# Layer 1's folded queries: a second level of Strassen in four of seven products, for seven of eight batch elements

## The chip, the cores and the metric

The kernel runs on one core of a Trainium2 chip. The metric is the device time of one execution in microseconds; the time before is the median of three runs. The profile is of one further execution. Everything is float32.

## The reference, cut to what matters

Two attention layers over eight images of 512 channels and 1024 pixels. The change touches layer 1:

```python
h = _group_norm(x, gamma, beta).reshape(B, C, N)          # C = 512, N = 1024
q = jnp.einsum('oc,bcn->bon', wq, h) + bq[None, :, None]
k = jnp.einsum('oc,bcn->bon', wk, h) + bk[None, :, None]
v = jnp.einsum('oc,bcn->bon', wv, h) + bv[None, :, None]
logits = jnp.einsum('bcn,bcm->bnm', q, k) * scale
attn = jax.nn.softmax(logits, axis=-1)
o = jnp.einsum('bnm,bcm->bcn', attn, v)
out = jnp.einsum('oc,bcn->bon', wp, o) + bp[None, :, None]
return x + out.reshape(B, C, H, W)
```

Layer 0 is a layer norm over channels, attention with eight heads of 64, an output projection and the residual.

## The kernel before

**Folded weights.** In layer 1 the product wq^T wk is formed once ("a") and the keys are h itself: the queries qa are one 512 x 512 matrix times h, plus a vector `ua`. Values and output projection are folded as well ("m").

**Strassen.** Each large product is one level of Strassen: a matrix is four blocks of 256 rows, with the sums S1 to S4 of the weights and T1 to T4 of the operands (Winograd's form). `STEPS` gives the order of the seven products and the bank that each goes to; a step with False adds onto what is in the bank:

```python
STEPS = [("11", "11", "x", True), ("12", "21", "z", True), ("S2", "T2", "x", False), ("S1", "T1", "y", True),
         ("S3", "T3", "x", False), ("S4", "22", "y", False), ("22", "T4", "x", False)]
```

`Product` runs them: `multiply()` puts matmuls on TensorE; `leave()` then copies x or y out (ScalarE, before the next step adds onto it) or adds a bank and a copy into the result (VectorE, `out`, L386). So steps 0, 2, 3 and 6 end in a copy u(0, 0), u(0, 1), u(1, 1) or the block (1, 0), and steps 1, 4 and 5 in an out. Between the two, `step()` calls `tick(pieces)`.

**A second level.** The scores (`Whole.scores`, L1160) are `SINGLES`, six outer products, each of them seven inner ones of 128 x 128 x 512 by the same steps, and the seventh outer product (22 with T4, L1195) whole. They run as three pairs of units. Inner sums of the operands are made by `deep_operands_later` (L558 to L563), those of the queries by `Whole.deep_query` (L1134 to L1140). Layer 0's keys and queries are done likewise (`project_deep`, L588), with inner sums of the weights made once, saved to DRAM (`save_deep_later`) and loaded for each element (`load_deep`).

**The queries before.** `project` makes two units, one for each 128 rows of a block. Each of the seven products is whole: 4 matmuls of 128 x 128 x 512 in all, 2 to a unit (L481). In between, two steps of the next element's layer-0 values (unit `n_units[1]`, L490) take the time in which group norm and the T sums are made (`meanwhile`).

**Order.** PE, ACT, DVE and POOL run their instructions in the order in which the program is written; DMAs on SP have a queue of their own. POOL can run ahead of the others where nothing holds it. Work that has no fixed place goes through one first-in first-out queue of closures, `side`: `later()` puts entries at its end, a `tick` runs one, and `until()` runs entries until what is needed exists. Which step an entry lands in is a matter of counting.

**From scores to the softmax's sums.** After each pair of scores, entries add the outer products together (`adds`, L1200), `finish` takes the exponentials of a block (L1148), `key_sum` adds its two halves on VectorE (L1250), `more_sums` adds the other blocks by accumulating DMAs of POOL (L1255), and `fold` folds the 128 partitions by further ones (L720, L716). `inverse` turns them on VectorE (L724) and spreads the rows on ScalarE (L1294). The next element's layer norm goes on behind it (L797). While this runs, the folded values (`project_v`, x_vm, y_vm, z_vm, L490) and the product with the attention (x_o, y_o, z_o, L506) are on TensorE, and the v units take the ticks (2, 2, 2, 2, 1, 1, 1) and (1, 1, 1, 2, 1, 2, 2).

**Stores.** `put_away` stores the next element's layer-0 values to DRAM (v_away), `residual` adds the folded output bias to the residual x1 on ScalarE (L1538) and stores it (x_away, L1539). `LayerNorm.sums` adds the next but one input over its channels by POOL's DMAs (L753). All tiles of 4 KB a partition come from one pool of 46.

Of the kernel before, what the change touches and what calls it, by code (L numbers as in the profile page):

```python
# [20 lines left out]
P = 128  # L21
# [50 lines left out]
def fast_path(ctx: ExitStack, tc: tile.TileContext, x: bass.AP, vecs: dict, weights: dict, out: bass.AP,  # L72
# [139 lines left out]
    saved_deep = {n: dram.tile([P, 3, 2, 4, P], F32, tag=f"saved_deep_{n}", name=f"saved_deep_{n}") for n in ("k", "q")}  # L212
# [4 lines left out]
    def load_deep(n, b):  # L217
        ready = {}
        for g in range(3):
# [5 lines left out]
    def save_deep_later(n, w):  # L225
# [18 lines left out]
        for g in range(3):  # L244
            sums(g)

    def save_w(n, w):
# [99 lines left out]
    def later(*work):  # L347
        side.extend(work)
# [198 lines left out]
    def operand_inner(h, deep, names):  # L547
# [2 lines left out]
        return Inner(blocks, lambda: [{t: deep[x][:, i] for i, t in enumerate(order)} for x in names],  # L550
                     lambda: all(x in deep for x in names))

    def deep_operands_later(h, deep, names):

        def first(n):
            x = h[n]
            t = made[n] = big_tile(f"{n}_deep_{h['tag']}").rearrange("p (i t) -> p i t", i=4)
            nc.vector.tensor_sub(t[:, :2], x[:, :, CB:], x[:, 0, :].rearrange("p (n t) -> p n t", n=2))  # L558

        def rest(n):  # L560
            x, t = h[n], made[n]
            nc.vector.tensor_add(t[:, 2], t[:, 1], x[:, 0, :CB])
            nc.vector.tensor_sub(t[:, 3], x[:, 1, :CB], t[:, 2])  # L563
            deep[n] = t

        made = {}
        for n in names:
            later(lambda n=n: first(n), lambda n=n: rest(n))

    def project_deep(tag, w, w_deep, bias, h, h_deep, pieces):  # L570
# [44 lines left out]
        def run():  # L615
# [47 lines left out]
            res["last"] = last  # L663
            yield
        return run(), res

    def rows_of(t, c, k):

# [443 lines left out]
    class Whole:  # L1112
# [3 lines left out]
        def __init__(self, b, qa, hb, x1):  # L1116
            self.b, self.hb, self.x1 = b, hb, x1
            self.q_deep = {}
            self.pieces = (2, 2, 1)
            self.q = {f"{i + 1}{j + 1}": qa[j, i] for i in range(2) for j in range(2)}  # L1120
# [5 lines left out]
            for n in names:  # L1126
                sum_later(self.q, n, lambda n: block(f"{n}_qa_{self.b}"), wide)

        def deep_query(self, *names):
# [12 lines left out]

            made = {}
            for n in names:
                later(lambda n=n: first(n), lambda n=n: rest(n))

# [3 lines left out]
        def scores(self, h_deep):  # L1150
# [51 lines left out]
            def adds(ts_, xs):  # L1202
                later(*(lambda g=g: add(ts_[g], xs[g]) for g in range(2)))

            def finish(n, t):
                def exponentials():
                    for g in range(2):
                        self.exponential(t[g])
                    self.p[n] = t
                later(exponentials)  # L1210

            for j in range(3):
                units = [unit(2 * j + n) for n in range(2)]
                for i in range(len(STEPS)):
                    for u in units:
                        u.multiply()
                    copy = plain(j, i - 3) if j < 2 and i in (3, 4) else nothing
                    tick(self.pieces[j])
                    for u in units:
                        u.leave()  # L1220
                    copy()
                m1, m2, m3, m5, m4, m7 = made
                if j == 0:
                    adds(m2, m1)
                    finish("11", m2)
                elif j == 1:
                    self.key_sum(0, "11")
                    adds(m3, m1)
                    adds(m5, m3)
                    adds(whole6, m5)  # L1230
                    finish("12", whole6)
                else:
                    adds(m3, m4)
                    adds(m7, m3)
                    self.key_sum(1, "12")
                    later(lambda: add(m5[0], m4[0]))
                    finish("21", m7)
# [148 lines left out]
    with tc.manual_schedule(engines=ORDERED):  # L1386
# [62 lines left out]
        for u in units:  # L1449
            u.pieces = 2  # L1450
            u.rest()
        save_deep_later("q", wq_now)
        units, vts = project_v("v0", wv_now, hb)
        for u in units:
            u.pieces = 2
            u.rest()
        for b in range(B):
# [51 lines left out]
            o_units[1].step(2)  # L1509
            o_units[0].rest()  # L1510
            wa_now = load_w("a", b)
            gn = GroupNorm(b, x1, stats)
            if not more:
                until(lambda: not side)
# [19 lines left out]
            def residual(i, k):  # L1534
# [3 lines left out]
                    nc.scalar.activation(t[:, r, :], t[:, r, :], AF.Identity, bias=bm[:, oc : oc + 1])  # L1538
                nc.sync.dma_start(out=x1_away[i, k], in_=wide(t))  # L1539
            h1b = operands(h1)  # L1540
            if more:
                add_operands(h1b)
            a_units, qa = project(f"qa{b}", wa_now, lambda oc: ua[:, oc : oc + 1], h1b,
                                  own="x" if more else "")
            if not more:
# [8 lines left out]
            a_units[0].step(1)  # L1554
            meanwhile(3)
            a_units[0].step(1)
            if more:
                vn_away = {ik: put_away(t, f"v_away_{b + 1}_{ik[0]}{ik[1]}") for ik, t in vn.items()}
            a_units[1].step(2)
            ln = LayerNorm(b + 2) if b + 2 < B else None  # L1560
            if ln:
                ln.sums()
            h1_deep = {}
            away = list(x1)
            for n, (_, name) in enumerate(SINGLES):
                deep_operands_later(h1b, h1_deep, [name])
                later(*(lambda ik=ik: residual(*ik) for ik in away[n : n + 1]))
            for u in a_units:
                u.pieces = 2
            a_units[0].rest()  # L1570
            whole = Whole(b, qa, h1b, x1_away)
            whole.deep_query("11")
            a_units[1].step(5)
            whole.deep_query("12")
            whole.query_sum("S1", "S2")
            whole.deep_query("S2")
            whole.query_sum("S3")
# [445 lines left out]
```

## Time and profile before

| | |
|---|---|
| Median of three runs | 2820.01 us (2818.68 to 2821.12) |
| Profiled execution, its own time | 2816.65 us |
| Its span | 2814.4 us |
| Granted TensorE clock | 1.00 |
| PE busy | 2801.8 us |
| DVE busy | 2066.1 us |
| ACT busy | 1233.8 us |
| POOL busy | 502.0 us |
| One element's queries, element 0 | from 280.44 to 307.92 us |
| Its scores | from 307.92 to 351.05 us |

Times in the rows of the profile are microseconds from the span's start; in the groups' rows the mean duration is in ns. Matmuls overlap in the records, so what one costs is read from the distance between starts. A float32 matmul leaves two records, each with a weight load on PEld.

### The profile page before, as it was taken

To read this page: it belongs to the slowest core of one execution; us is meant where nothing else is said; L and a number is where in the kernel's file an instruction comes from. 1 tells how busy PE (TensorE), PEld (TensorE's weight loads), DVE (VectorE), ACT (ScalarE), POOL (GpSimd) and SP (SyncE) were. 2 spreads that over 40 slices of the span, in tenths; PEclk is the share of its full clock that TensorE was granted. 3 is DMA by queue.
4 is the path that set the end of the run, shared out by engine and by line. 5 is a ranking of instruction groups with operands and counts; after the bars stand their busy time and mean duration, and the time that the engine had idled before them with its cause. 6 is when DMAs were issued, how large, how long until landed. Compare 5 with 4: busy or idle time off the path is not lost.

```text
span 2814.4 us, 31060 instructions
## 1 busy us (share of the span) xinstructions
PE 2801.8 (100%) x10807; PEld 1596.2 (57%) x10807; DVE 2066.1 (73%) x2892; ACT 1233.8 (44%) x2079; POOL 502.0 (18%) x685
## 2 busy tenths in 40 slices
PE   9999999999999999999999999999999999999999
PEld 5535656357553575535854457644676346663375
DVE  6677777777767776777767777678767777657785
ACT  4463435724257242662436523365234733236341
POOL 2021022210222102220032200222012210122001
PEclk9999999999999999999999999999999999999999
DMA  8234267352663527535374353734337432372214
GB/s 315 93 82 110 79 166 185 68 131 86 156 170 72 144 82 182 128 78 165 89 188 96 91 152 92 200 78 114 123 98 202 99 85 86 71 206 63 65 64 99
DMA packets 133765, 341.38 MB, mean 121 GB/s; under 512 B 18928, under 2 KB 23328, under 8 KB 133600
## 3 DMA queue, kind: packets, MB, share of 16 engines
q0 software_dynamic: 53760, 127.45, 24.7%
q1 hardware_dynamic: 79744, 211.84, 21.1%
q8 instruction: 87, 1.43, 0.2%
q14 instruction: 78, 0.64, 0.1%
q10 hardware_dynamic: 96, 0.02, 0.0%
HBM read 190.87 MB, written 62.39 MB: 90 GB/s over the span
## 4 chain that ended last, share of the span: by engine, by line
PE 94%; DMA 3%; DVE 1%; issue 1%; ACT 0%; POOL 0%; ACTq 0%; POOLq 0%; DVEq 0%
PE s L1003 16%; PE acc L1021 16%; PE s L1160 7%; PE x_o L506 6%; PE x_v L490 4%; PE x_qa L481 4%; PE x_out L481 4%; PE x_vm L490 3%; PE y_s L1160 3%; PE y_o L506 3%; PE y_v L490 2%; PE y_out L481 2%; PE s L1195 2%; PE x_q L588 2%; PE y_qa L481 2%; PE y_vm L490 2%
## 5 line engine op out<-in xcount | busy, mean ns | idle before, releaser
L1012 DVE TENSOR_TENSOR sum<-sum,p 128x1024 f32<-128x1024 f32 x384 | 470.4, 1225 | 39.4 <-DVE sum L1012 1.4
L1006 ACT ACTIVATE p<-s 128x1024 f32<-128x1024 f32 (+1 forms) x608 | 478.9, 983 | 15.1 <-PE s L1003 15.1
L1021 PE MATMUL acc<-p,v_again 128*64 128x512 f32 x1792 | 390.9, 594 | 0.0
L1021 PEld LDWEIGHTS acc<-p,v_again 128*64 128x64 f32 x1792 | 126.1, 137 | 261.4 <-issue 236.7
L716 POOL DMA_DIRECT2D fold<-sum x312 | 207.6, 757 | 302.4 <-DMA sum<-sum 187.0
L1003 PE MATMUL s<-q,k 64*128 64x512 f32 x1152 | 252.2, 592 | 0.0
L1003 PE MATMUL s<-q_lower,k_lower 64*128 64x512 f32 x896 | 196.1, 592 | 0.0
L1010 DVE TENSOR_TENSOR sum<-p,p 128x1024 f32<-128x1024 f32 x64 | 78.1, 1221 | 157.8 <-ACT p L1006 157.8
L1003 PEld LDWEIGHTS s<-q,k 64*128 64x128 f32 x1152 | 109.6, 186 | 138.4 <-issue 84.6
L1255 POOL DMA_DIRECT2D sum<-p x32 | 28.5, 970 | 864.6 <-PE y_vm L490 757.2
L1003 PEld LDWEIGHTS s<-q_lower,k_lower 64*128 64x128 f32 x896 | 85.4, 186 | 110.5 <-issue 68.5
L720 POOL DMA_DIRECT2D sum<-sum x78 | 66.2, 849 | 419.1 <-DVE sum L1012 239.6
L1025 ACT COPY o<-acc 128x512 f32<-128x512 f32 x63 | 36.9, 586 | 221.2 <-PE acc L1021 221.0
L1200 DVE TENSOR_TENSOR p<-p,p 128x1024 f32<-128x1024 f32 x112 | 131.7, 1216 | 0.0
L506 PE MATMUL x_o<-T_p,S_vm 128*128 128x512 f32 x256 | 115.2, 592 | 0.0
L511 ACT COPY u(0, 0)_v<-x_v 128x512 f32<-128x512 f32 x16 | 9.4, 586 | 186.5 <-PE x_v L490 186.5
L490 PE MATMUL x_vm<-w_m,T_gn 128*128 128x256 f32 x384 | 90.7, 379 | 0.0
L481 PE MATMUL x_qa<-T_gn,w_a 128*128 128x512 f32 x192 | 89.4, 594 | 0.8 <-ACT qa L524 0.8
L481 PE MATMUL x_out<-T_o,w_o 128*128 128x512 f32 x192 | 89.2, 594 | 0.0
L506 PEld LDWEIGHTS x_o<-T_p,S_vm 128*128 128x128 f32 x256 | 48.6, 190 | 60.7 <-issue 60.7
L1067 ACT COPY rr<-r 32x16 f32<-32x16 f32 x256 | 53.5, 209 | 62.4 <-DVE r L970 59.0
L490 PE MATMUL x_v<-w_v,T_h 128*128 128x256 f32 x336 | 80.0, 381 | 0.0
(524 smaller groups left out, 5317.9 us busy)
## 6 DMA issues: line engine op xcount, KB each, us to landing
sum<-sum POOLq DMA_DIRECT2D x78, 256.0 KB, 3.4
fold<-sum POOLq DMA_DIRECT2D x312, 64.0 KB, 2.4
x<-in_x_dram SPq DMA_DIRECT2D x32, 512.0 KB, 5.4
xr<-in_x_dram SPq DMA_DIRECT2D x64, 256.0 KB, 5.0
x_away<-x SPq DMA_DIRECT2D x32, 512.0 KB, 2.7
sum<-p POOLq DMA_DIRECT2D x32, 512.0 KB, 5.9
v_away<-v SPq DMA_DIRECT2D x28, 512.0 KB, 3.3
v_again<-v_away SPq DMA_DIRECT2D x28, 512.0 KB, 9.2
```

The costliest lines, as they stand in the source:

```text
L481: nc.tensor.matmul(dst, a[:, k, ts(r, P)], b[:, k, :], start=(opens and k == 0), stop=(k == 1), skip_group_check=True)
L490: nc.tensor.matmul(dst[:, ts(m, CB)], b[:, k, ts(2 * r + m, P)], a[:, k, :], start=(opens and m == 0 and k == 0), stop=(k == 1), skip_grou ...
L506: nc.tensor.matmul(dst, a[:, m, ts(r, P)], b[m // 2][:, m % 2, :], start=(opens and m == 0), stop=(m == NM // 2 - 1), skip_group_check=True)
L716: nc.gpsimd.dma_start(out=f[ts(q + i, BL), :], in_=t[ts(n, BL), ts(i, HB)], accum_op=ALU.add if n else ALU.bypass)
L720: nc.gpsimd.dma_start(out=t[:D, :], in_=t[D:, :], accum_op=ALU.add)
L1003: nc.tensor.matmul(parts[i], self.k[m // 4][r, ts(m % 4, P)], self.q[r, :], start=True, stop=True)
L1006: nc.scalar.activation(dst, src, AF.Exp, scale=1.0 / float(D) ** 0.5)
L1010: nc.vector.tensor_add(self.sum, self.p[0], p)
L1012: nc.vector.tensor_add(self.sum, self.sum, p)
L1021: nc.tensor.matmul(acc[i * D : (i + 1) * D, :], value_of(self.vt, m, self.c * P + i * D, D), self.p[m][:, ts(i, HB)], start=(m == 0), stop ...
L1160: nc.tensor.matmul(dst[:, ts(c, CB)], x[0][:, ts(c, P)], a[0], start=(opens and c == 0), stop=True, skip_group_check=True)
L1200: nc.vector.tensor_add(wide(t), wide(t), wide(x))
```

## The change

For elements 0 to 6 the queries go through a new `project_mixed`. Three outer products stay whole (m1 = 11 with 11, m2 = 12 with 21, m6 = 22 with T4); the other four (S2 with T2, S3 with T3; S1 with T1, S4 with 22) are done as two units of two, each outer product by seven inner ones of 128 x 128 x 256. The order on every engine is written out in it. The inner sums of the operands, which the scores need as well, are made here (`Primes`), and the residual's stores are placed here (`beside`). The last two blocks of the queries (22 and 21) are summed by entries of `side` (`closing`). Inner sums of the weights S1, S2, S3, S4 are made once, saved, and loaded for each element. In the scores of all eight elements, the sums of the first pair go to POOL's DMAs, and the exponentials of block 11 and its key sum change their place. Element 7 keeps `project`.

```diff
+        for g in groups:
...
+    class Primes:
+        def __init__(self, h):
+            self.h, self.deep = h, {}
+        def first(self, n):
+            x = self.h[n]
+            t = self.deep[n] = big_tile(f"{n}_deep_{self.h['tag']}").rearrange("p (i t) -> p i t", i=4)
+            nc.vector.tensor_sub(t[:, :2], x[:, :, CB:], x[:, 0, :].rearrange("p (n t) -> p n t", n=2))
+            nc.vector.tensor_add(t[:, 2], t[:, 1], x[:, 0, :CB])
+        def last(self, n):
+            t = self.deep[n]
+            nc.vector.tensor_sub(t[:, 3], self.h[n][:, 1, :CB], t[:, 2])
...
+    def project_mixed(tag, w, w_deep, bias, h, primes, between, away, beside, ready):
+        n_blocks = {n: block(f"{tag}_{n}") for n in ("m1", "m2", "m6")}
+        banks = {n: wide_psum(f"{n}_{tag}") for n in "cab"}
+        made = [[None, None], [None, None]]
+        def products(n, r, t):
+            a, x = {"m1": ("11", "11"), "m2": ("12", "21"), "m6": ("22", "T4")}[n]
+            for k in range(2):
+                nc.tensor.matmul(banks[t][:, ts(r, HB)], w[a][:, k, ts(r, P)], h[x][:, k, :], start=(k == 0),
+                                 stop=(k == 1), skip_group_check=True)
+        def biased(n, r, t, i):
+            nc.scalar.activation(n_blocks[n][:, r, :], banks[t][:, ts(r, HB)], AF.Identity, bias=bias(2 * i + r))
+        def part(dst, a, x, opens):
+            for s in range(2):
+                nc.tensor.matmul(dst[:, ts(s, CB)], a[s], x[s], start=(opens and s == 0), stop=True,
+                                 skip_group_check=True)
...
+        def step(u, *work):
+            u.multiply()
+            for x in work:
+                x()
+            u.leave()
...
+            later(lambda: sums(c22, "22", q22), nothing, nothing, nothing, lambda: sums(c12, "21", q21))
+        def c12(r):
+            nc.vector.scalar_tensor_tensor(q21[:, r], mc[r][:, 1], bias(r), mb[r][:, 0], ALU.add, ALU.add)
+        def c22(r):
+            nc.vector.scalar_tensor_tensor(q22[:, r], mc[r][:, 0], bias(2 + r), mb[r][:, 1], ALU.add, ALU.add)
+        products("m1", 0, "c")
+        add_operand(h, "T1")
+        between()
+        add_operand(h, "T2")
+        products("m1", 1, "c")
+        beside()
+        add_operand(h, "T3")
+        between()
+        nc.scalar.copy(wide(n_blocks["m1"]), banks["c"])
+        away()
+        primes.first("T2")
+        primes.first("T3")
+        beside()
+        for r in range(2):
+            products("m2", r, "b")
+        biased("m2", 0, "b", 0)
+        B, C_ = unit(0), unit(1)
+        m1, m2, m6 = (n_blocks[n] for n in ("m1", "m2", "m6"))
+        primes.first("T1")
+        primes.first("22")
+        primes.last("T2")
+        primes.last("T3")
+        step(B)
+        biased("m2", 1, "b", 0)
+        nc.gpsimd.dma_start(out=wide(m2), in_=wide(m1), accum_op=ALU.add)
+        step(B)
+        step(B, t("T4"))
+        beside()
+        step(C_, last("T1", "22"))
+        step(B, first("21"))
+        step(C_, last("21"))
+        beside()
+        step(B)
+        step(C_, first("11"), last("11"))
+        step(B)
+        products("m6", 0, "c")
+        biased("m6", 0, "c", 1)
+        step(B, lambda: ready(m2))
+        step(C_)
+        mb, mc = made
+        step(C_)
+        pairs(lambda r: add(mb[r][:, 0], m1[:, r]))()
+        products("m6", 1, "c")
+        biased("m6", 1, "c", 1)
+        step(C_, pairs(lambda r: add(mb[r][:, 1], mb[r][:, 0])), pairs(lambda r: add(m6[:, r], mb[r][:, 1])))
+        step(C_)
+        for r in range(2):
+            nc.gpsimd.dma_start(out=mb[r][:, 0], in_=mc[r][:, 0], accum_op=ALU.add)
...
                 if j == 0:
-                    adds(m2, m1)
+                    for g in range(2):
+                        nc.gpsimd.dma_start(out=wide(m2[g]), in_=wide(m1[g]), accum_op=ALU.add)
+                elif j == 1:
                     finish("11", m2)
-                elif j == 1:
-                    self.key_sum(0, "11")
                     adds(m3, m1)
                     adds(m5, m3)
                     adds(whole6, m5)
+                    self.key_sum(0, "11")
                     finish("12", whole6)
...
             wa_now = load_w("a", b)
+            if more:
+                wa_deep = load_deep("a", b, (1, 2))
...
+                def vn_put_away():
+                    for ik, t in vn.items():
+                        vn_away[ik] = put_away(t, f"v_away_{b + 1}_{ik[0]}{ik[1]}")
+                    if ln:
+                        ln.sums()
...
+                def ready(t):
+                    whole.q["11"] = t
+                    whole.query_prime("11")
+                qa, closing = project_mixed(f"qa{b}", wa_now, wa_deep, lambda oc: ua[:, oc : oc + 1], h1b, primes,
+                                            lambda: n_units[1].step(1), vn_put_away,
+                                            lambda: residual(*spare.pop(0)), ready)
+                whole.q["12"] = qa[1, 0]
+                whole.deep_query("12")
+                closing(whole.q)
```

More of the change, by code (lines that the diff above doesn't have):

```diff
@@ L210, in load_w, with load_deep @@
         return w
-    saved_deep = {n: dram.tile([P, 3, 2, 4, P], F32, tag=f"saved_deep_{n}", name=f"saved_deep_{n}") for n in ("k", "q")}
+    saved_deep = {n: dram.tile([P, 3, 2, 4, P], F32, tag=f"saved_deep_{n}", name=f"saved_deep_{n}") for n in ("k", "q", "a")}
     def deep_tile(n, b, g):
         return big_tile(f"w_{n}_{b}_{g}_deep").rearrange("p (s i o) -> p s i o", s=2, i=4)
-    def load_deep(n, b):
+    def load_deep(n, b, groups=range(3)):
         ready = {}
-        for g in range(3):
+        for g in groups:
             deep = deep_tile(n, b, g)
@@ L223, in load_deep, with save_deep_later @@
         return ready
-    def save_deep_later(n, w):
+    def save_deep_later(n, w, groups=range(3)):
         def sums(g):
@@ L242, in sums @@
                   lambda: nc.gpsimd.dma_start(out=saved_deep[n][:, g], in_=made[0]))
-        for g in range(3):
+        for g in groups:
             sums(g)
@@ L665, in project_deep, with unit, dest, bank_of @@
         return run(), res
+    def project_mixed(tag, w, w_deep, bias, h, primes, between, away, beside, ready):
[13 more added lines that the diff above has]
+                                 skip_group_check=True)
+        def unit(j):
+            def dest(i, k):
+                if made[j][i] is None:
+                    made[j][i] = big_tile(f"{tag}_{j}{i}").rearrange("p (s t) -> p s t", s=2)
+                return made[j][i][:, :, ts(k, CB)]
+            def bank_of(to):
+                if to == "y":
+                    return bank(f"y_{tag}_{j}")
+                return banks["c"][:, ts(j, HB)] if to == "z" else banks["ab"[j]][:, :HB]
+            a, x = ((("S2", "S3"), ("T2", "T3")), (("S1", "S4"), ("T1", "22")))[j]
+            u = Product(f"{tag}_{j}", weight_inner(w, w_deep, a), operand_inner(h, primes.deep, x), part, plain_shift,
+                        dest, bank_of)
+            u.view = lambda t: t.rearrange("p (s t) -> p s t", s=2)
+            return u
+        def step(u, *work):
[3 more added lines that the diff above has]
+            u.leave()
+        def t(n):
+            return lambda: add_operand(h, n)
+        def first(n):
+            return lambda: primes.first(n)
+        def last(*names):
+            return lambda: [primes.last(n) for n in names]
+        def add(dst, src):
+            nc.vector.tensor_add(dst, dst, src)
+        def pairs(work):
+            return lambda: [work(r) for r in range(2)]
+        def closing(q):
+            def sums(f, n, t):
+                for r in range(2):
+                    f(r)
+                q[n] = t
+            later(lambda: sums(c22, "22", q22), nothing, nothing, nothing, lambda: sums(c12, "21", q21))
[49 more added lines that the diff above has]
+        step(C_)
+        for r in range(2):
+            nc.gpsimd.dma_start(out=mb[r][:, 0], in_=mc[r][:, 0], accum_op=ALU.add)
+        q21, q22 = (block(f"{tag}_{n}") for n in ("21", "22"))
+        return {(1, 0): m6}, closing
@@ L1119, in __init__ @@
             self.pieces = (2, 2, 1)
-            self.q = {f"{i + 1}{j + 1}": qa[j, i] for i in range(2) for j in range(2)}
+            self.q = {f"{i + 1}{j + 1}": qa[j, i] for i in range(2) for j in range(2) if (j, i) in qa}
             self.p = {f"{j + 1}{k + 1}": [None, None] for j in range(2) for k in range(2)}
@@ L1127, in query_sum, with query_prime, query_primes @@
                 sum_later(self.q, n, lambda n: block(f"{n}_qa_{self.b}"), wide)
-        def deep_query(self, *names):
+        def query_prime(self, n):
+            first, rest = self.query_primes()
+            first(n)
+            rest(n)
+        def query_primes(self):
             def first(n):
@@ L1143, in deep_query @@
             made = {}
+            return first, rest
+        def deep_query(self, *names):
+            first, rest = self.query_primes()
             for n in names:
@@ L1452, in fast_path @@
         save_deep_later("q", wq_now)
+        save_deep_later("a", wa, (1, 2))
         units, vts = project_v("v0", wv_now, hb)
@@ L1540, in fast_path @@
             h1b = operands(h1)
+            ln = LayerNorm(b + 2) if b + 2 < B else None
+            primes = Primes(h1b)
+            h1_deep = primes.deep
             if more:
[L1542 to L1545, printed above, removed]
+                def vn_put_away():
[3 more added lines that the diff above has]
+                        ln.sums()
+                vn_away = {}
+                spare = list(x1)
+                whole = Whole(b, {}, h1b, x1_away)
+                def ready(t):
[7 more added lines that the diff above has]
+                closing(whole.q)
+            else:
+                a_units, qa = project(f"qa{b}", wa_now, lambda oc: ua[:, oc : oc + 1], h1b, own="")
                 h1b["T1"] = t1
@@ L1553, in fast_path @@
                 add_operands(h1b)
[L1554 to L1574, printed above, removed]
+                a_units[0].step(2)
+                a_units[1].step(2)
+                away = list(x1)
+                for n, (_, name) in enumerate(SINGLES):
+                    deep_operands_later(h1b, h1_deep, [name])
+                    later(*(lambda ik=ik: residual(*ik) for ik in away[n : n + 1]))
+                for u in a_units:
+                    u.pieces = 2
+                a_units[0].rest()
+                whole = Whole(b, qa, h1b, x1_away)
+                whole.deep_query("11")
+                a_units[1].step(5)
+                whole.deep_query("12")
             whole.query_sum("S1", "S2")
```

## The prediction

> **What bounds the kernel now.** I read the page first (engines, then the 40 slices), then the order of time around the queries of element 0, then the waits of TensorE, then the chain that follows the layer-1 scores.
>
> ```profile
> span 2814.4 us, 31060 instructions
> ...
> PE 2801.8 (100%) x10807; PEld 1596.2 (57%) x10807; DVE 2066.1 (73%) x2892; ACT 1233.8 (44%) x2079; POOL 502.0 (18%) x685
> ...
> PEclk9999999999999999999999999999999999999999
> ```
>
> TensorE has 12.6 us of gaps in 2814.4, at full clock: only less matmul time, or a new wait, can move the end. Two shapes matter (a float32 matmul leaves two records):
>
> ```profile
> 292.47 1.88 PE L481 MATMUL y_qa<-T_gn,w_a 128*128 128x512 f32 x4
> 294.19 1.88 PE L481 MATMUL x_qa<-T_gn,w_a 128*128 128x512 f32 x4
> ...
> 307.92 3.62 PE L1160 MATMUL s<-qa,gn 128*128 128x256 f32 x16
> 311.38 1.03 PE L1160 MATMUL s<-11_deep_qa,11_deep_gn 128*128 128x256 f32 x4
> ```
>
> Durations overlap; starts do not. Four records of 512 columns take 294.19 - 292.47 = 1.72 us, 0.429 each; sixteen of 256 take 311.38 - 307.92 = 3.46, 0.216 each.
>
> Where an engine is 100% busy, the thinnest cover is what to look for. It is behind the scores: the softmax sums go through POOL's DMAs, one waiting for another.
>
> ```profile
> 358.26 0.91 POOL L1255 DMA_DIRECT2D sum<-p  x1 [84.59 <-PE y_vm L490]
> 365.08 1.77 POOL L1255 DMA_DIRECT2D sum<-p  x2 [5.90 <-PE x_vm L490]
> 374.18 0.87 POOL L1255 DMA_DIRECT2D sum<-p  x1 [7.32 <-DMA sum<-p]
> ...
> 388.33 1.61 POOL L716 DMA_DIRECT2D fold<-sum  x2 [1.41 <-DMA fold<-sum]
> ```
>
> ```profile
> 391.61 0.71 DVE L724 STREAM_TRANSPOSE fold1t<-fold 128x512 f32<-128x512 f32 x1 [1.70 <-DMA fold<-sum]
> ```
>
> ```profile
> 394.13 1.70 ACT L1294 COPY rr<-r 32x16 f32<-32x16 f32 x8 [0.91 <-DVE r L970]
> 395.88 1.70 ACT L797 COPY lnmur<-lnm 32x16 f32<-32x16 f32 x8
> 397.60 0.59 ACT L511 COPY u(1, 1)_o<-y_o 128x512 f32<-128x512 f32 x1
> ```
>
> ```profile
> PE y_k L588 <- ACT u(1, 1)_k L602: 1.2, 2, 1.0
> ...
> PE y_o L506 <- ACT u(1, 1)_o L511: 0.4, 1, 0.4
> ```
>
> VectorE stands idle for the folds; the copy u(1, 1)_o comes behind the sums' rows on ScalarE and ends at 398.2, and TensorE adds onto that bank at 399.25: 1.1 us to spare. The same rows of the other elements give 0.35 (element 1), 1.1 (3), 2.0 (6), 2.6 (7); in 2, 4 and 5 TensorE already waits for it (0.2, 0.6, 0.0). Thirty us on, y_k waits for a half tile freed by a store of the same chain: spare 0, 0.2, 0, 1.1, 0, 0, 1.7 in elements 0 to 6. So in five of eight elements this DMA chain has nothing to spare, or next to nothing.
>
> **The change, part by part.**
>
> *TensorE.* Per element, four products of 8 records leave, 32 x 0.429 = 13.73 us; four inner Strassens of 7 matmuls of 256 columns come, 28 x 2 x 0.216 = 12.10. Saved 1.64 us, x 7 = 11.5. Layer 0, scores, values and element 7's queries keep their matmuls. A rule speaks against this. Each 256-column record has its own weight load of 190 ns in the profile, so 24 more loads per element. The Trainium skill, "TensorE: Matmul & The Clock Gate", says under "The mechanism" that a load overlaps running matmuls only when its row group differs, and under "LDWEIGHTS (loading the stationary operand)" that it takes columns / 1.2 GHz. Estimated from that page: 24 x 107 ns = 2.6 us per element, a loss of 0.9 x 7 = 6.5 us instead. The rows at 307.92 and 311.38 change weights in every record, use the full 128 rows, and still start 216 ns apart; I take the rows.
>
> *VectorE, in the query stage.* It has 27.48 us now and 25.84 after. After, VectorE carries four T sums at 1.22 (4.9), six deep operands of 0.68 + 0.42 + 0.42 (9.2 with gaps closed), six outs at 0.69 (4.1), one out of v (0.7), query_prime of 11 (1.5) and six sums of 512 columns at 0.68 (4.1): 24.5, after 1.7 us of group norm. Laid out in its order against TensorE's, it reaches the last out 2 us after TensorE reaches the scores (in the page 0.9, by the copy of qa). Inside the stage no operand is late: T2's first half is ready 3 us before its product, out(1,1) of the second unit 1.6 us before the bank is used again. The scores start with query 12 (m6), whose first half is summed 0.2 us before its matmul. In the scores the tightest bank (z, read by out(0,0)) is asked for 6.9 us in: 2 us of lag, 1.5 deep query, 1.5 c22, 0.7 out make 5.7. If that cover goes, each us of lag costs 7 us in all.
>
> *ScalarE.* One 1.0 us copy and four biased copies of 0.69 more per element; it is busy 10.9 of 27.5. One tight spot: unit B runs steps 0, 1, 2 alone, so its copy of x has one step of 0.86 us: 0.2 latency + 0.59 + release. Cost 0 to 0.05 each, I take 0.3 us in all.
>
> *DMAs and queues.* POOL gets m2 += m1 (512 KB), triggered 12.7 us into the stage, and VectorE reads it 7.3 us later, with 1.2 us more before the matmuls feel it. Nearest row: sum<-p, 4.6/5.9/10.4 us to landing. At 5.9 it is hidden; at 10.4 it costs 1.9 once. Behind it on POOL stand two 256 KB adds (3.4 us in row sum<-sum), due 5 us later. The two adds of m2 and m1 in the scores move from VectorE (2 x 1.22) to POOL and have 15 us. On SP, two loads of 512 KB join w_a at about 250 (w_k_deep: 7.4 us) and are read at 292; behind them v_away waits for results until 275.8 anyhow. The first residual store now goes ahead of v_away, whose reader comes an element later. The residuals (2 x 0.66 on ScalarE) end earlier than at present. Once, at the start: 8 sums of 0.68 and two POOL DMAs under layer 0's attention, where TensorE waits for exponentials only: 0.
>
> *Work that moves: the step that costs.* The side queue gets five entries more (closing). Of its 19 entries the first pair of scores takes 14, the second takes 5 and runs dry; exponentials of 11, formerly done there, follow it. The third pair has 7 ticks, as before, for 9 entries, not 8: two are left instead of one. So exponentials of 21, the eighth entry of the next stage, become the ninth: from the fourth step (two ticks) of the first v unit to the fifth. On ScalarE that puts them behind the copy of the fourth step, here:
>
> ```profile
> 356.43 0.59 ACT L511 COPY u(0, 1)_vm<-x_vm 128x512 f32<-128x512 f32 x1 [2.22 <-PE x_vm L490]
> 356.91 2.00 ACT L1148 ACTIVATE p<-p 128x1024 f32<-128x1024 f32 x2
> 358.82 0.58 ACT L511 COPY u(1, 1)_vm<-y_vm 128x512 f32<-128x512 f32 x1
> ```
>
> Copies of consecutive steps are 1.73 us apart, so they start at 358.6, and with them POOL's chain, 1.7 us late against TensorE. How much arrives at the end is not in the trace. Above: all 1.7, since each DMA waits for the last. Below: the first leg takes 6.3 us beside loads of x, 4.6 to 4.8 in elements 6 and 7 without; if the late start escapes them, 0.1 arrives. I take 1.0, the middle. By the spare times above it costs 1.0 in elements 0, 2, 4, 5 and 0.8 in 1: 4.8 us (0.4 at 0.1; 9.0 at 1.7). Here too a rule differs: "DMA: Bandwidth & Descriptors", "Anatomy of one DMA", gives 2.0 us + bytes / 436e3, an estimated 3.2 us for 512 KB. With that the chain's three long legs (6.3, 8.0, 5.8) would end 10 us sooner and nothing be given back. The rows decide.
>
> *Sum.* -11.5 + 0.3 + 4.8 = -6.4. The profiled execution took 2816.65 (span 2814.4 and 2.25 around it), so 2810.3 for its like; the median of the three runs is 3.4 above it, which I keep: 2820.0 - 6.4 = 2813.6.
>
> **The rivals.**
>
> *A. All of it stays.* The late chain catches up in contention: -11.5 + 0.3 + 0.4 = -10.8, 2809.2. For it: the first leg is 1.5 us shorter where no x is loaded (elements 6, 7). Against: three elements already wait, and the last two loads of x wait for sums that come a tick later as well.
>
> *B. Most is given back.* The full 1.7 us arrives: -2.2, 2817.8; no difference that shows.
>
> *C. Slower: the column sums of the next input hold POOL's queue.* m2 += m1 stands behind them. In element 0 they run from 237 to 275, 37 us, as each add waits for the last. Their tile takes a place freed by attention; the change takes more tiles before it. Were it a place freed by the output projection (266), they would end at 303, m2 land at 309, VectorE stand before query_prime, and TensorE lose 7 us in six elements: -6.4 + 43, 2856. It decides once the sums start after about 260. Against: counting in order, only one more tile is taken ahead of it, and its place is freed at the same time.
>
> *D. The matmuls do not shrink as said* (loads show): about 2826.
>
> **How the numbers follow.** Main case (2811 to 2816) 0.45, A (2807.5 to 2811) 0.27, B (2816 to 2819) 0.20, C and D together 0.08. About 0.2% (5.6 us, 2814.4) is what a measurement of this kernel can tell from no change. Of the main case four fifths lie below: 0.36, with A 0.63, and 0.02 for gains of which I see nothing: faster 0.65. Same: B and the rest of the main case, 0.28. Slower 0.07. The range for 8 in 10 runs from 2808 to 2818.
>
> **What would show it.** PE busy should fall by some 6 us, gaps and all; the 392 records of x_qa, y_qa and z_qa at L481 in elements 0 to 6 give way to 168 of 512 columns and 392 of 256, and these should start 0.216 apart. exponentials of 21 should come after u(1, 1)_vm, POOL's first sum<-p 52 instead of 50.3 us into the scores, and the waits for u(1, 1)_o and u(1, 1)_k should grow from 1.6 to some 6 us. VectorE should go straight from query outs into 12_deep_qa without TensorE waiting. I am wrong if TensorE waits inside the query stage, for m2 or for m6, or if the chain comes no later.

## The result, and the profile after

| | median of runs, us | profiled execution: own span, us |
|---|---|---|
| before | 2819.4 (2815.3 to 2827.6, 22 runs) | 2814.4 |
| changed | 2815.0 (2811.3 to 2819.0, 22 runs) | 2809.9 |

The ratio of the times is 0.9984, 95% interval 0.9977 to 0.9990: 4.4 us faster, where 6.4 were forecast and 2808 to 2818 was the range. Measured again beside other kernels it gave 0.9986 (0.9979 to 0.9993). The two spans differ by 4.5 us, as the medians do, so the traces can be set against each other. Both profiled executions lie under the median of their kernel, by 2.7 and 3.4 us, so each has probably somewhat less waiting than a usual one.

The page of the changed kernel, its engines:

```profile
span 2809.9 us, 31744 instructions
...
PE 2792.2 (99%) x10975; PEld 1627.0 (58%) x10975; DVE 2092.7 (74%) x2954; ACT 1249.2 (44%) x2114; POOL 534.9 (19%) x724
...
PEclk9999999999999999999999999999999999999999
```

TensorE is busy 9.6 us less, and its gaps went from 12.6 to 17.7 us (2809.9 - 2792.2): the matmuls were saved, and about half of the saving came back as waiting. TensorE's groups show the new mix: three groups of 56 records of 512 columns (168), and records of 256 columns, 392 in all groups of L701 together.

```profile
L693 PE MATMUL c_qa<-gn,w_a 128*128 128x512 f32 x56 | 26.3, 592 | 0.0
L693 PE MATMUL c_qa<-T_gn,w_a 128*128 128x512 f32 x56 | 26.3, 592 | 0.0
L693 PE MATMUL b_qa<-gn,w_a 128*128 128x512 f32 x56 | 25.2, 592 | 0.0
L701 PE MATMUL a_qa<-T_deep_gn,w_a_deep 128*128 128x256 f32 x56 | 14.9, 389 | 0.0
```

Their order in time, in the query stage of element 0 (start, length with overlaps, line, operands, records):

```profile
291.42 1.03 PE L701 MATMUL a_qa<-T_gn,w_a 128*128 128x256 f32 x4
292.28 1.03 PE L701 MATMUL c_qa<-T_gn,w_a 128*128 128x256 f32 x4
293.15 1.10 PE L701 MATMUL a_qa<-T_deep_gn,w_a_deep 128*128 128x256 f32 x4
...
307.02 3.62 PE L1309 MATMUL s<-qa_m,gn 128*128 128x256 f32 x16
```

From 291.42 to 292.28 four records start, 0.215 us each, with a weight load in front of each one. The third row is 1.10 long where its neighbours are 1.03: there TensorE waits 0.08 us for the copy of the first unit's bank on ScalarE, which ends at 293.07. The stage runs from 281.10 to 307.02, 25.92 us, against 27.49 before: 1.57 us less in each of seven elements.

Now the other side, the waits of TensorE (us in total, times, longest). Before, these two lines had 1.6 us together; now they have 6.4:

```profile
PE y_o L506 <- ACT u(1, 1)_o L511: 4.0, 4, 1.7
PE y_k L604 <- ACT u(1, 1)_k L618: 2.4, 4, 0.9
```

Here, in order of time, is what stands ahead of them in element 0 (scores' start 307.02): first ScalarE, then POOL, then the end of the chain on VectorE, ScalarE and TensorE:

```profile
355.53 0.59 ACT L511 COPY u(0, 1)_vm<-x_vm 128x512 f32<-128x512 f32 x1 [2.22 <-PE x_vm L490]
357.31 0.59 ACT L511 COPY u(1, 1)_vm<-y_vm 128x512 f32<-128x512 f32 x1 [1.19 <-PE y_vm L490]
357.79 2.01 ACT L1297 ACTIVATE p<-p 128x1024 f32<-128x1024 f32 x2
```

```profile
359.14 0.87 POOL L1405 DMA_DIRECT2D sum<-p  x1 [33.76 <-ACT p L1297]
365.40 1.77 POOL L1405 DMA_DIRECT2D sum<-p  x2 [5.38 <-ACT u(0, 0)_vm L511]
375.32 0.87 POOL L1405 DMA_DIRECT2D sum<-p  x1 [8.16 <-ACT vm L511]
...
390.40 1.61 POOL L856 DMA_DIRECT2D fold<-sum  x2 [1.41 <-DMA fold<-sum]
```

```profile
393.62 0.71 DVE L864 STREAM_TRANSPOSE fold1t<-fold 128x512 f32<-128x512 f32 x1 [4.61 <-DMA fold<-sum]
```

```profile
399.61 0.59 ACT L511 COPY u(1, 1)_o<-y_o 128x512 f32<-128x512 f32 x1
```

```profile
400.25 1.98 PE L506 MATMUL y_o<-p,S_vm 128*128 128x512 f32 x4 [1.73 <-ACT u(1, 1)_o L511]
```

The exponentials of 21 (357.79) now stand behind the copy u(1, 1)_vm. POOL's first sum<-p starts 52.12 us into the scores (before: 50.34). The last two folds are issued from 390.40 on, 83.4 us into the scores (before: 80.4). TensorE stands 1.73 us for the copy of u(1, 1)_o.

Measured from start to start of the matmuls, the 4.5 us of the two spans are made up like this (without waiting, an element's output projection of layer 1 takes 48.07 us, the keys and queries of the next element 43.22; what is above that is waiting):

| part | before | changed | difference |
|---|---|---|---|
| queries, elements 0 to 6 | 7 x 27.49 | 7 x 25.92 | -11.0 |
| waits for the folds in the output projection, elements 0 to 6 | 1.2 | 5.1 | +3.9 |
| waits for the half tile in the key projection | 1.9 | 3.5 | +1.6 |
| first column sums, at 18 us | 1.3 | 2.0 | +0.7 |
| last element's end, one score stage, rounding | | | +0.3 |
| sum | | | -4.5 |

The fourth row is not the change's: it is the same code in every kernel here, and its four records take between 1.0 and 2.1 us from one trace to another (the last section shows why).

### The profile page after: what moved, and what is told of

Read it like the earlier page. It is cut to its first block, busy times and chain, and to the rows that moved or that the text cites. A ratio compares the mean times of both kernels' runs of the same rounds, so it can differ in the third digit from the quotient of the medians.

```text
span 2809.9 us, 31744 instructions
## 1 busy us (share of the span) xinstructions
PE 2792.2 (99%) x10975; PEld 1627.0 (58%) x10975; DVE 2092.7 (74%) x2954; ACT 1249.2 (44%) x2114; POOL 534.9 (19%) x724
## 5 line engine op out<-in xcount | busy, mean ns | idle before, releaser
L1349 DVE TENSOR_TENSOR p<-p,p 128x1024 f32<-128x1024 f32 x96 | 114.7, 1224 | 6.3 <-ACT p L511 6.3
L490 PEld LDWEIGHTS x_vm<-w_m,T_gn 128*128 128x128 f32 x384 | 72.8, 190 | 10.0
```

The costliest lines, as they stand in the source:

```text
L490: nc.tensor.matmul(dst[:, ts(m, CB)], b[:, k, ts(2 * r + m, P)], a[:, k, :], start=(opens and m == 0 and k == 0), stop=(k == 1), skip_grou ...
L1349: nc.vector.tensor_add(wide(t), wide(t), wide(x))
```

## The experiments

The theory: the matmuls bring 11 us, and 5.5 to 7 of these are given back because one more entry in the third pair's side work makes the exponentials of 21 a step later, with them POOL's chain of accumulating DMAs, and behind it the copy that TensorE waits for. The rivals: the new transfers crowd the queues; VectorE is late; the matmuls do not bring what their records say.

Each is compared with the kernel before, run on the same chip: three chips in all, on which its medians were 2819.3, 2818.5 and 2818.8 us.

| run | median, us (runs) | ratio to before, 95% interval |
|---|---|---|
| delay alone, on the kernel before | 2826.6 (11) | 1.0027 (1.0018 to 1.0036) |
| new DMA order, on the kernel before | 2814.8 (21) | 0.9983 (0.9977 to 0.9990) |
| new DMA order, on the changed kernel | 2818.8 (13) | 1.0000 (0.9992 to 1.0008) |
| three pieces in the first step | 2815.0 (21) | 0.9984 (0.9977 to 0.9990) |
| exponentials first | 2809.9 (5) | 0.9963 (0.9949 to 0.9977) |
| scores' hunk undone | 2815.8 (21) | 0.9989 (0.9983 to 0.9996) |
| the same, new DMA order | 2813.1 (11) | 0.9980 (0.9971 to 0.9989) |
| that with new DMA order, m2 += m1 on VectorE | 2818.9 (13) | 0.9999 (0.9990 to 1.0007) |
| entries at the front | 2807.2 (5) | 0.9955 (0.9941 to 0.9968) |
| entries at the front, new DMA order | 2802.9 (5) | 0.9943 (0.9930 to 0.9957) |
| changed kernel again | 2814.4 (18) | 0.9986 (0.9979 to 0.9993) |

**1. The delay alone.** Onto the kernel before, nothing of the change but an empty entry:

```diff
                 else:
+                    later(nothing)
                     adds(m3, m4)
```

> The kernel before, with one empty entry put into the side queue ahead of the sums of the third pair of scores: exponentials of 21 become the ninth entry, as in the change, and nothing else of the change is in it. Theory: POOL's first sum<-p starts 1.7 us later, and the waits grow from 3 to 7 to 9 us: 4 to 6 us slower than the kernel before. Rival (the late start is absorbed, and the waits of the changed kernel come from its new transfers): no difference.

It costs 7.3 us. The exponentials of 21 stand behind u(1, 1)_vm and the first sum<-p starts 52.12 us into the scores (which begin at 308.41), as in the changed kernel:

```profile
358.70 0.59 ACT L511 COPY u(1, 1)_vm<-y_vm 128x512 f32<-128x512 f32 x1 [1.20 <-PE y_vm L490]
359.18 2.00 ACT L1148 ACTIVATE p<-p 128x1024 f32<-128x1024 f32 x2
```

```profile
360.53 0.91 POOL L1256 DMA_DIRECT2D sum<-p  x1 [86.15 <-PE x_vm L490]
```

The waits are the same two (from start to start 13.7 us in this trace, 7.5 of them in one element whose transfers were slow; before 3.1):

```profile
PE y_o L506 <- ACT u(1, 1)_o L511: 7.0, 4, 4.3
PE y_k L588 <- ACT u(1, 1)_k L602: 1.8, 3, 0.9
```

So one empty entry, with none of the new transfers or sums, costs as much as the change lost: -11.0 + 7.3 = -3.7, and -4.4 was measured. The interval of this run is 5 to 10 us, so by itself it does not exclude a small cost of the new transfers beside the delay. The seventh experiment keeps those of the query stage, and there the time falls by the whole saving of the matmuls: these at least cost nothing that shows.

**2. An earlier start, first try.** On the changed kernel, the first step of the first v unit does three pieces:

```diff
-            for u, pieces in zip(v_units, ((2, 2, 2, 2, 1, 1, 1), ...
+            for u, pieces in zip(v_units, ((3, 2, 2, 2, 1, 1, 1), ...
```

> The changed kernel, with one number changed: the first step of the first v unit does three pieces of side work, not two, so that exponentials of 21 and 22 come one step earlier, where they were before the change. Theory (the late exponentials are what is given back): POOL's first sum<-p starts 50.3 us into the scores instead of 52.1, the waits for u(1, 1)_o and u(1, 1)_k shrink from 6.4 us to 2 or less, and the time is 4 to 5 us below the changed kernel's, 9 us below the kernel before. Rival 1 (the new transfers and the moved residual stores crowd the DMA queues, and the late start is of no account): the chain ends as late as in the changed kernel, the time stays 4 us below the kernel before. Rival 2 (VectorE is late with the sums, not the order of ScalarE): the exponentials start no earlier, same time as rival 1.

The time did not move (2815.0), and yet neither rival is right. The chain did start at 50.34, and the waits in the output and key projections fell from 8.6 to 3.0 us. But a new line leads the waits:

```profile
PE x_vm L490 <- DVE vm L386: 3.6, 8, 0.5
```

The third piece puts one more sum of 1.2 us on VectorE ahead of the outs of the v stage; that stage takes 25.25 us instead of 24.17 in each of eight elements, 8.6 us. From start to start, 0.24 us of an element's loss is a wait for the copy u(1, 1)_vm, which stands behind exponentials that wait for VectorE's sums, and most of the rest is the wait for the out. The expectation counted the gain and forgot that VectorE is full there.

**3. An earlier start, second try.** Exponentials of 21 change places with two sums that they don't need:

```diff
-                    self.key_sum(1, "12")
-                    later(lambda: add(m5[0], m4[0]))
                     finish("21", m7)
+                    self.key_sum(1, "12")
+                    later(lambda: add(m5[0], m4[0]))
```

> The changed kernel with exponentials of 21 queued ahead of the second key sum and of m5 += m4, so that they are the seventh entry and run in the fourth step of the first v unit, as before the change, with no step doing more than two pieces; exponentials of 22 stay as late as in the change (they gate only the later transfers). Theory: VectorE's order of work in the v stage is not made heavier ahead of the first sums, so the 1.1 us per element that the run with three pieces in the first step lost there are not lost; POOL's first sum<-p starts at 50.3 us, the waits of the output projections fall from 8.6 us (start to start, trace of the changed kernel) to 3, and the time is 5 us below the changed kernel, 9 to 10 below the kernel before. Rival (the chain's end is set by its later legs, whatever the start): waits stay at 6 to 9, 4 us below the kernel before.

The median is 2809.9: 8.6 us below the kernel before, where the changed kernel is 4.4 below it, so 4.2 us gained of the 5 that the theory has. But these are five runs with a wide interval, and the profiled one, the slowest of the five (2813.2), bears the theory out only in part. The start is at 50.70. The v stage takes 24.52 us, 0.35 more in each element: the exponentials wait for VectorE's sums, and u(1, 1)_vm is copied behind them, 0.5 us later than before the change. The waits are 7.7 us, hardly below 8.6: in that execution the first transfer took 6.8 us on average instead of 5.4. By itself this run settles nothing.

**4. The chain made shorter.** Four transfers add to two sums; in both kernels their order is sum 0, 0, 1, 1, so that the second chain stands on POOL behind the first one's wait. The edit makes it 0, 1, 0, 1:

```diff
-                    later(lambda: self.more_sums(0, "21"))
+                    later(lambda: self.more_sum(0, "21", 0))
...
-                    side.insert(len(side) - 1, lambda: (self.more_sums(1, "22"), self.fold()))
+                    side.insert(len(side) - 1, lambda: (self.more_sum(1, "22", 0), self.more_sum(0, "21", 1),
+                                                        self.more_sum(1, "22", 1), self.fold()))
```

On the kernel before:

> The kernel before, with the same new order of the four accumulating transfers and nothing of the change. Theory: the waits for u(1, 1)_o and u(1, 1)_k (3.1 us by start to start in the trace of before) go to zero, 3 us below the kernel before. Its distance to the run with the same order in the changed kernel is then the pure saving of the matmuls, 10.5 to 11. Rival (the rule that a weight load does not overlap): that distance is near zero or has the other sign.

It is 4.5 us faster: its waits for u(1, 1)_o are gone, and of those for u(1, 1)_k 0.5 us are left in one element. On the changed kernel:

> The changed kernel, with the four accumulating transfers of the softmax sums in the order (sum 0, sum 1, sum 0, sum 1) instead of (0, 0, 1, 1): each of the two chains then waits only for its own. The exponentials stay late. Theory (the chain of POOL's DMAs is all that is given back, and gave the waits of the kernel before as well): the folds end some 6 us earlier, both waits go to zero, the time is the matmuls' saving and the old waits together: 11 + 3 = 14 us below the kernel before, less a few tenths for the tight copy in the query stage: 13 to 14. Rival (contention: two transfers at once take twice as long each): the folds end no earlier, 4 us below the kernel before.

Its median is 3.8 us above the changed kernel's. The expectation missed where the exponentials of 22 stand: they too had moved, from 51.56 to 55.90 us into the scores. The second transfer needs them:

```profile
359.14 0.87 POOL L1405 DMA_DIRECT2D sum<-p  x1 [33.76 <-ACT p L1297]
364.26 1.77 POOL L1405 DMA_DIRECT2D sum<-p  x2 [4.25 <-PE x_vm L490]
369.39 0.87 POOL L1405 DMA_DIRECT2D sum<-p  x1 [3.36 <-DMA sum<-p]
373.27 0.81 POOL L860 DMA_DIRECT2D sum<-sum  x1 [3.00 <-DMA sum<-p]
382.38 0.80 POOL L860 DMA_DIRECT2D sum<-sum  x1 [8.30 <-DMA sum<-p]
```

```profile
367.60 3.77 SPq L209 DMA_DIRECT2D w_k<-saved_k  x3
```

The first transfer for 22 starts at 57.25 in place of 52.9 us into the scores, and the last of the four, issued at 369.39 into the three loads of w_k (60.6 to 64.4), takes until 382.1 to land, 12.7 us. The same order that frees the chain in one kernel ties it up in the other, because there it waits for a later producer.

**5. The scores' part undone.** m2 += m1 on VectorE after the first pair and exponentials of 11 behind it, as before; the query stage stays changed:

```diff
                 if j == 0:
-                    for g in range(2):
-                        nc.gpsimd.dma_start(out=wide(m2[g]), in_=wide(m1[g]), accum_op=ALU.add)
-                elif j == 1:
-                    finish("11", m2)
+                    adds(m2, m1)
+                    finish("11", m2)
+                elif j == 1:
+                    self.key_sum(0, "11")
                     adds(m3, m1)
...
-                    self.key_sum(0, "11")
```

> The changed kernel with the scores' hunk as before and nothing else altered: seven second-level query products stay. Theory (one more entry among the third pair's, which the hunk makes by moving exponentials of 11 there, is the whole of the give-back): exponentials of 21 at 49.0 us again, waits as in the kernel before (3 us start to start), 11 us below the kernel before, 2808 to 2809. Rival (the give-back comes from the new entries of the query stage in the side queue, or from the transfers): 4 to 7 us below the kernel before.

> The changed kernel with the scores' hunk as before (m2 += m1 on VectorE right after the first pair, exponentials of 11 after it, the first key sum ahead of the sums of m3), and the four accumulating transfers in the order 0, 1, 0, 1. Theory: exponentials of 21 and 22 are back at 49.0 and 51.6 us, all waits for the folds are gone as in the kernel before with that order (2814.8), and what is left of the difference to it is the query stage alone: 7 x 1.57 = 11 us, 2804, 15 below the kernel before. Rival (the change loses somewhere else too, in VectorE's stages or the DMA queues): 2807 to 2811.

Both miss. The waits for the folds went as expected: 2.7 us are left in the first run, about as many as in the kernel before, and none with the new order. But the scores take 1.1 to 2.3 us longer in each of seven elements, 9.1 us in all:

```profile
PE s L1344 <- ACT p L1346: 7.2, 7, 1.9
```

In order of time, ScalarE in the scores of element 0:

```profile
330.05 2.13 ACT L1297 ACTIVATE p<-p 128x1024 f32<-128x1024 f32 x2 [1.67 <-DVE p L1349]
332.09 1.05 ACT L511 COPY u(1, 1)_s<-y_s 128x512 f32<-128x512 f32 x2
333.04 0.60 ACT L1346 COPY p<-s 128x512 f32<-128x512 f32 x1
```

The queue is five entries longer, so the exponentials of 11, appended behind it, run at 23.2 us into the scores instead of 17.9, just ahead of three copies that free PSUM banks. So the hunk of the scores is no mistake: it takes these 2 us of ScalarE out of a place where they cost 9.1 us over the run, and puts them where they cost 5.5.

**6. VectorE's margin in the query stage.** On the run with the hunk undone and the new order, the inner sum by VectorE:

```diff
-        nc.gpsimd.dma_start(out=wide(m2), in_=wide(m1), accum_op=ALU.add)
+        nc.vector.tensor_add(wide(m2), wide(m2), wide(m1))
```

> As the run with the scores' hunk as before and the order 0, 1, 0, 1, and the sum m2 += m1 inside the query stage by VectorE (one instruction of 1024 columns, 1.2 us) where the change has a transfer on POOL. VectorE stands idle for 0.8 and 1.6 us in that stage of the changed kernel's trace, behind that place. Theory of the prediction (VectorE has just room): the 1.2 us go into the second of these gaps and the time is the same within 1 us. Rival (VectorE is at its limit): the sums of the first unit come 1.2 us late, its bank is not free, and each of seven elements loses 0.5 to 1.2 us, 3.5 to 8 us in all.

It is 5.8 us slower by the medians than the same kernel with the transfer (3.7 between the two profiled executions), as the rival has it. The 1.2 us do go into VectorE's idle 1.6, but on the way the second unit's first out, which m6 waits for, ends 18.3 us into the stage instead of 16.9 (the query stage takes 26.25 us instead of 25.92), and in some elements the scores take longer too, up to 1.5 us. VectorE has no room there, though it stands idle for 2.4 us of the stage.

**7. Everything in its old place.** The two sums and the exponentials of 11 go to the front of the queue after the first pair, so that the five new entries are what waits:

```diff
                 if j == 0:
+                    queued = len(side)
                     adds(m2, m1)
                     finish("11", m2)
+                    side.rotate(len(side) - queued)
```

> The same with the four transfers in their order as in both kernels, 0, 0, 1, 1. Theory: scores and folds as in the kernel before, whose waits (3 us) stay: 11 us below it, 2808. Rival (as above): 2811 or more.

> The changed kernel with m2 += m1 on VectorE and exponentials of 11 at the front of the side queue after the first pair of scores, so that they run at 17.9 us into the scores as before the change and the five new entries are what waits; the first key sum ahead of the sums of m3 as before; the four accumulating transfers in the order 0, 1, 0, 1. Theory: the exponentials of 11 at 23.2 us, which cost 1.1 to 2.2 us an element in the two runs with the scores' hunk as before, are back in their old hole; those of 21 and 22 come at 49.0 and 51.6; no waits for the folds; the difference to the kernel before with that order (2814.8, 4.5 below before) is the query stage, 11 us: 2804, 15 below the kernel before. Rival (five more entries make another of the scores' copies or sums late): 2808 or more.

> The changed kernel once more, beside the two others on the same chip. Theory: 4 to 5 us below the kernel before, 6 to 7 above the run with the order as in both kernels, 10 to 11 above the one with the order 0, 1, 0, 1; o and k projections wait 5 to 9 us in its profile.

The medians are 2807.2, 2802.9 and 2814.4, all within 1.2 us of what was expected. With the order 0, 1, 0, 1 neither wait is left: the scores, the v stage and both projections have their usual lengths in every element, but for 0.2 us in one score stage. POOL's chain in element 0 (scores' start 306.69 on this clock):

```profile
357.03 0.87 POOL L1406 DMA_DIRECT2D sum<-p  x1 [46.56 <-PE y_vm L490]
359.60 0.87 POOL L1406 DMA_DIRECT2D sum<-p  x1 [1.70 <-ACT p L1297]
362.96 0.87 POOL L1406 DMA_DIRECT2D sum<-p  x1 [2.50 <-DMA sum<-p]
365.81 0.87 POOL L1406 DMA_DIRECT2D sum<-p  x1 [1.99 <-issue]
...
385.16 1.61 POOL L856 DMA_DIRECT2D fold<-sum  x2 [1.41 <-DMA fold<-sum]
```

The last two folds are issued from 385.16 on, 5 us earlier against the scores' start than in the changed kernel, and ScalarE has the exponentials ahead of u(1, 1)_vm again:

```profile
355.68 2.00 ACT L1297 ACTIVATE p<-p 128x1024 f32<-128x1024 f32 x2
357.58 0.57 ACT L511 COPY u(1, 1)_vm<-y_vm 128x512 f32<-128x512 f32 x1
```

This version beats both kernels: it is 16 us below the one before, 11.5 below the changed one beside it, both far beyond the scatter of its five runs (2802.4 to 2804.9). And it isolates the matmuls: the same order of transfers on the kernel before gave 4.5 us, so 11.4 are the rest, of which the query stages make 11.0.

## Why the prediction was right, point by point

*TensorE.* 1.64 us per element were forecast, 1.57 measured; over seven, 11.5 and 11.0. The rule weighed against it does not hold here: the Trainium skill, "TensorE: Matmul & The Clock Gate", "The mechanism", would have put an estimated 2.6 us of weight loads on each query stage, with the load time that its section "LDWEIGHTS (loading the stationary operand)" gives. The stage is 25.92 us long, 0.08 more than its records' columns take, and that 0.08 is a wait for a copy. PE busy fell by 9.6 us, where some 6 were foreseen: the 6 was the change of the whole span, and busy time leaves out the new gaps.

*ScalarE's tight copy.* 0.08 us per element instead of 0 to 0.05: 0.55 us for the 0.3 taken. This is the whole difference between 1.64 and 1.57.

*VectorE.* Its last query out ends 1.7 us behind the scores' start (2 forecast), and the scores are not held up, but for 0.1 us in element 4. That the cover is thin was right: 1.2 us more for each of seven elements cost 5.8 over the run in the sixth experiment. One detail was misread: by the order in the program the scores start with query 11, and query 12 (m6) comes four records later, at 307.88, 0.3 us behind the end of its first half's sum (307.54). VectorE's order after the last products (start, length, line, operands):

```profile
306.85 1.29 DVE L737 TENSOR_TENSOR qa_m<-qa_m,qa 128x512 f32<-128x512 f32 x2
308.05 0.68 DVE L386 TENSOR_TENSOR qa<-u(0, 1)_qa,y_qa 128x512 f32<-128x512 f32 x1
308.65 0.42 DVE L1279 TENSOR_TENSOR 12_deep_qa<-qa_m 128x256 f32<-128x256 f32 x1
```

*The transfer of m2 += m1, and rival C.* One row answers both:

```profile
293.95 0.91 POOL L780 DMA_DIRECT2D qa_m<-qa_m  x1 [19.82 <-ACT qa_m L697]
```

It starts 12.85 us into the stage, lands after 4.7 and is read after 6.7, so it is hidden; in all seven elements it starts at the same place and lands within 5.8. POOL had stood idle for 19.8 us before it (17.8 or more in the other elements) and was released by ScalarE, so the column sums of the next input did not hold its queue.

*The step that costs.* The mechanism is the one described: the exponentials of 21 as the ninth entry, behind u(1, 1)_vm, and a start at 52.1. The first experiment shows it by itself. Of a lateness of 1.7 us (measured: 1.8), 1.0 was taken to arrive at the end, the middle between two ends and not worked out. The last fold of elements 0 to 5 lands 84.26 us into the scores before, on average, and 85.34 in the changed kernel (85.45 in the second trace of it): 1.1 us later. That the middle came so near is luck. As foreseen, the first transfer, started later, takes less: 5.4 us on average instead of 6.3. That it is the loads of x that it escapes was not tried. The cost was put at 4.8 us, with 0.4 and 9.0 as ends; it is 5.5 in this trace, 5.8 in the second, 6.6 by the medians (11.0 - 4.4), 7.3 when the delay is put on alone. So this term was 1 to 2 us too small, and that is most of the distance between the -6.4 forecast and the -4.4 measured.

*What it had wrong within that term.* The cost was spread evenly, 1.0 in elements 0, 2, 4 and 5. In the trace the chain ends 3.0 us later in element 0 and 2.7 in element 3, and within 0.5 of its old end in all the others; elements 0 and 3, with 1.1 us to spare, took most of the new waiting in the output projection (2.0 and 1.6 us). In the second trace of the same kernel most of it is in elements 1, 3 and 5. How long a transfer takes changes from run to run (element 0's first: 5.7 us in one trace, 4.6 in the other). An average shift of 1.1 with a scatter of more than a microsecond can cost more than an even shift of 1.0, since what comes early gains nothing; that this is why the cost was larger is argued, not tried.

*What it didn't see.* The exponentials of 22 move by 4.3 us, more than those of 21, because the steps behind the fourth take one piece each. In the changed kernel this costs nothing: their transfer stands behind the first chain anyway, and starts at 57.8 or later where they would allow it at 57.25. But it decided the run with the new order.

*The rivals.* A (all of it stays) and B (most is given back) were the ends of one distribution, and the result, 2815.0, lies in the main case (2811 to 2816), on the side of B. C is answered above, and D is out.

## What to carry to other kernels

When a kernel's side work is a queue that is drained so many pieces per step, adding entries moves everything behind them: count which long instruction of an engine falls into which step, and let the new entries wait, not the old ones.

A chain of dependent DMAs that ended just ahead of its reader turned 1.8 us of lateness at its head into 5 to 7 us over this run. Guarding its start was worth 7.2 us (2814.4 to 2807.2), and issuing its two independent halves alternately another 4.4; the second pays only if each half's input is ready when its turn on the queue comes, as the run on the changed kernel shows.

An engine that is idle for 2.4 us of a stage need not have room for an instruction of 1.2 us: look at what stands behind the place where it would go.

## What the runs showed of the hardware that was not expected

Two accumulating transfers of 512 KB to different tiles, started 2.6 us apart, each took about as long as one alone. In the fastest kernel the first takes 5.9 us on average over elements 0 to 5 and the second, beside it, 6.0; with the old order the first takes 6.1 alone. Started 0.55 us apart, as the second and third of the old order are, they did not share so evenly: 4.6 and 6.6 us in element 7 of the kernel before. Issued just behind the second of three loads of w_k, the fourth transfer took 11.6 to 12.7 us (elements 0 to 5 of the changed kernel with the new order); with the entries at the front it is issued about when these loads start, or ahead of them, and took 5.9 to 6.6.

The first column sums are two products of 64 columns, two records each, and take 1.0 to 2.1 us from trace to trace. What decides it is when the second product's operand is ready. In every trace its first record starts 0.05 to 0.14 us after VectorE's last sum of that operand, and the four records end 1.0 us after that. VectorE's sum, in turn, comes behind a load of the input x. The changed kernel's trace (2.0 us):

```profile
17.81 1.22 DVE L905 TENSOR_TENSOR lns<-x,x 128x1024 f32<-128x1024 f32 x1 [2.53 <-DMA x<-in_x_dram]
19.07 0.69 DVE L909 TENSOR_TENSOR lns<-lns 128x512 f32<-128x512 f32 x1
```

```profile
18.81 2.08 PE L900 MATMUL mean<-lns,ones_c 128*64 128x512 f32 x4
```

In the fastest kernel's trace the sum ends at 19.35, before either product starts:

```profile
19.48 1.08 PE L900 MATMUL mean<-lns,ones_c 128*64 128x512 f32 x4
```

There both products start within 0.01 us and take 1.0 us together, as long as one of them takes when they run one after the other. So two products that fill only 64 columns of the array each ran side by side.
